# A mixture of experts written as 32 turns in a fixed order, its norms by a power on GpSimd, and an output projection booked one turn later

## The chip, the cores and the metric

The kernel runs on one core of one Trainium2 chip, alone. The metric is the device time of one execution in microseconds (us). Before the change three runs took 4461.84, 4466.29 and 4487.71 us; the median is 4466.29 us. All arithmetic named here is float32.

## The reference, cut to what matters

The network takes 2 sequences of 1024 tokens with 128 features (T = 2048 tokens) and runs eight stages, each adding its result to a residual stream: windowed attention (a0), a mixture of experts (ffn0), causal attention (b0), the mixture of experts again with the same weights, a pair attention (a1), then a six-layer local-attention transformer (ffn1), another pair attention (b1), and ffn1 again. The change touches a0 and both ffn0 stages. Each ffn0 normalises its input and then computes:

```python
logits = xt @ gate_w.T
scores = softmax(logits)                      # 8 experts
top_vals, idx = top_k(scores, 2)
weights = take_along_axis(scores, idx)
xs = xt[:, None, :] * weights[:, :, None]
for e in range(8):
    mask = (idx == e)
    h  = silu(xs @ w1[e].T + b1[e])
    x2 = h @ w2[e].T + b2[e]
    x3 = xs @ w3[e].T + b3[e]
    y  = y + sum(x2 * x3 * mask)
z = (silu(xt @ sw1.T) * (xt @ sw2.T)) @ sw3.T # shared part, 256 wide
out = y + z
```

In a0 the reference has 16 heads of 8 features, windows of 64 queries against 128 keys, a softmax, and an output projection `out @ Wo.T + bo`. The norm in front of each stage is (x - mean) / sqrt(var + 1e-5).

## The kernel before, in words

The residual stream stays in SBUF, features on partitions, as four tiles `xt[0..3]` of 128 x 512 (512 tokens each, a "block"). A stage opens its own tile pools. The stages follow each other because each reads what the last one added to `xt`.

**ffn0.** Every expert is computed for every token; unchosen ones are scaled by zero. Four parts, all in `ffn0`:

1. For each of the four blocks: `norm` (L107) = `norm_in` (four transposes L115, statistics L119 and L120 on DVE, square root on ACT L126 and its reciprocal on DVE L127, scaling L130) and `norm_out` (transposes L139, copy to SBUF by ACT L142); then the gate logits of the block (L238).
2. The choice of two experts for all 2048 tokens at once: a chain of some twenty small DVE instructions with one exponential on ACT (L252 to L271) that leaves weights and marks in `sel`.
3. For each block: the rows of `sel` for the block are transposed (L278) and copied (L282); the shared part (`s1`, `s2` by L289, Silu L297, product L298, `yz` L299) is added to `xt` (L300).
4. For each block and each four experts: L306 spreads the four weights over 128 partitions by four matmuls with 32 rows each, into four PSUM banks; L310 multiplies them with the normalised block (`xe`). For each pair: L316 starts two banks with the b3 rows (again 32-row matmuls); then for each expert L321 adds w3, L289 makes h, L324 takes its Silu, L326 copies x3 to SBUF, L289 makes x2 from h, L328 (DVE) forms (x2 + b2) * x3, and L331 (GpSimd) adds it to `xt`. One block-and-expert is called a unit here; there are 32 in a stage.

All this is emitted in program order, but the order on each engine is the planner's: outside a manual schedule the framework places an instruction where its priorities and buffers allow, so the shared part of a later block and single spreads of L306 land between the experts of an earlier one. PSUM has eight banks: two pools of four ("m" and "tp"). The SBUF pool holds three buffers for h and for x3, six for xe.

**a0.** After the projections, `Chunks.run` walks 16 chunks of 128 queries in software-pipelined turns, inside a manual schedule: there PE, ACT, DVE and GpSimd execute exactly in the written order. Turn n holds both halves of the softmax of chunk n, the transposes of chunk n-2, the sums of n-1, the scores of n+1 and the outputs of n-2. In `outputs`, every fourth chunk (m % 4 == 3) also projects four finished chunks: matmuls L668 into `a0y`, and L670 on DVE adds the result to `xt`. The softmax's subtractions (L625, L626), L633 and L670 share DVE's queue in that order.

GpSimd's queue carries the normalisation of a0 (L636), the memset of `sel` (L251) and the 64 additions L331. SP's queue issues DMAs only, none of them inside these loops.

Of the kernel before, what the change touches and what calls it, by code (L numbers as in the profile page):

```python
# [10 lines left out]
F32 = mybir.dt.float32  # L11
BF16 = mybir.dt.bfloat16
AF = mybir.ActivationFunctionType
ALU = mybir.AluOpType
# [3 lines left out]
P = 128  # L18
# [28 lines left out]
class Net:  # L47
    def __init__(self, ctx, tc, t):
# [7 lines left out]
        self.nc.gpsimd.memset(self.eps, EPS)  # L56

# [53 lines left out]
    def norm_in(self, src, ps, key, tag="tp", by_exp=False):  # L111
        nc = self.nc
        tp = ps.tile([P, 4, P], F32, tag=tag, name=f"ln_in_{key}")
# [8 lines left out]
        if by_exp:  # L122
            nc.scalar.activation(rs, mv[:, :, 1], AF.Ln, bias=self.eps)
            nc.scalar.activation(rs, rs, AF.Exp, scale=-0.5)
        else:
            nc.scalar.activation(rs, mv[:, :, 1], AF.Sqrt, bias=self.eps)  # L126
            nc.vector.reciprocal(rs, rs)  # L127
        xn = self.lnp.tile([P, 4, P], F32, tag="ln_xn", name=f"ln_xn_{key}")
# [6 lines left out]
    def norm_out(self, xn, dst, ps, key, gain=None, bias=None, tag="tp"):  # L135
        nc = self.nc
        tq = ps.tile([P, 4, P], F32, tag=tag, name=f"ln_out_{key}")
# [78 lines left out]
    def ffn0(self, key):  # L216
        nc, tc = self.nc, self.tc
        NT = T // P
        with ExitStack() as ctx:
            cp = ctx.enter_context(tc.tile_pool(name=f"f0c_{key}", bufs=1))  # L220
            sb = ctx.enter_context(tc.tile_pool(name=f"f0s_{key}", bufs=3))
            ps = ctx.enter_context(tc.tile_pool(name=f"f0ps_{key}", bufs=4, space=PSUM))
            w, wsel = self.w["f0"], self.w["f0_sel"]
            w123 = w[:, 0 : 3 * E * P].rearrange("p (s e h) -> p s e h", s=3, e=E)
            o = 3 * E * P
            sw1, sw2, sw3 = (w[:, ds(o + 256 * i, 256)] for i in range(3))
            gate = w[:, ds(o + 768, E)]
            b1, b2 = w[:, ds(o + 776, E)], w[:, ds(o + 784, E)]
            desc = w[:, ds(o + 792, E)]
            spread, b3 = wsel[:, 0], wsel[:, 1]  # L230

            xn = []
            lg = ps.tile([P, NT, E], F32, tag="m", name=f"lg_{key}")
            for k in range(NBLK):
                x = cp.tile([P, 512], F32, tag=f"xn{k}", name=f"f0xn_{key}_{k}")
                self.norm(self.xt[k], x, ps, f"{key}_{k}")
                for c in range(4):
                    nc.tensor.matmul(lg[:, 4 * k + c, :], x[:, ts(c, P)], gate, start=True, stop=True)  # L238
                xn.append(x)


            def tl(name, shape=(P, NT, E)):
                return cp.tile(list(shape), F32, tag=name, name=f"{name}_{key}")

            def over_e(v):
                return v[:, :, None].to_broadcast([P, NT, E])

            s, m = tl("s"), tl("m", (P, NT))

            sel4 = tl("sel", (P, NT, 4, 32))  # L250
            nc.gpsimd.memset(sel4, 0.0)  # L251
            nc.vector.tensor_reduce(m, lg, AX.X, ALU.max)  # L252
            nc.vector.tensor_tensor(s, lg, over_e(m), ALU.subtract)
            nc.scalar.activation(s, s, AF.Exp)
            nc.vector.tensor_reduce(m, s, AX.X, ALU.add)
            nc.vector.reciprocal(m, m)
            nc.vector.tensor_tensor(s, s, over_e(m), ALU.mult)
            one, two, cand, rest = tl("one"), tl("two"), tl("cand"), tl("rest")
            dbc = desc[:, None, :].to_broadcast([P, NT, E])
            for left, hot in ((s, one), (rest, two)):  # L260
                nc.vector.tensor_reduce(m, left, AX.X, ALU.max)
                nc.vector.tensor_tensor(cand, left, over_e(m), ALU.is_equal)
                nc.vector.tensor_tensor(cand, cand, dbc, ALU.mult)
                nc.vector.tensor_reduce(m, cand, AX.X, ALU.max)
                nc.vector.tensor_tensor(hot, cand, over_e(m), ALU.is_equal)
                if hot is one:
                    nc.vector.scalar_tensor_tensor(rest, one, -4.0, s, ALU.mult, ALU.add)
            nc.vector.tensor_tensor(one, one, two, ALU.add)
            nc.vector.tensor_tensor(s, one, s, ALU.mult)
            for v, lo in ((s, 0), (one, E)):  # L270
                nc.vector.tensor_copy(  # L271
                    sel4[:, :, :, lo : lo + E], v[:, :, None, :].to_broadcast([P, NT, 4, E])
                )

            for k in range(NBLK):
                tp = ps.tile([P, 4, P], F32, tag="tp", name=f"f0ts_{key}_{k}")
                for c in range(4):
                    nc.tensor.transpose(  # L278
                        tp[:, c, :], sel4[:, 4 * k + c].rearrange("p r e -> p (r e)"), self.ident
                    )  # L280
# [3 lines left out]
                def bank(name, tag="m"):  # L284
                    return ps.tile([P, 512], F32, tag=tag, name=f"f0{name}_{key}_{k}")
# [940 lines left out]
```

## Time and profile before

| what | us |
|---|---|
| median of three runs | 4466.29 |
| the profiled execution, device time | 4471.09 |
| its span | 4469.3 |
| mean granted TensorE clock | 0.939 |
| a0's turns, from the first full turns to the last addition to `xt` | about 86 to 239.6 |
| first ffn0, from its first transpose to the first of b0 | 239.66 to 424.33 (184.7) |
| second ffn0, from its first transpose to the first of a1 | 519.31 to 704.35 (185.0) |
| busy in the span: PE, DVE, ACT, GpSimd | 3964.8, 3480.8, 2385.2, 1983.1 |

The two ffn0 stages are 370 of 4469 us; most of the rest is ffn1, which the change leaves alone. Times inside the span are counted from its start. PE busy time is the union of modelled matmul intervals, so a busy PE isn't a PE at its fastest; distances from start to start of matmuls tell more. A float32 matmul of 512 columns shows as two records (two passes). "Idle before" names what ended the wait of an engine.

### The profile page before, as it was taken

The numbers are of one execution on the slowest core, as the hardware profiler recorded it, in microseconds if no ns is written. First come the engines' busy times: TensorE is split into PE (matmuls) and PEld (weight loads), VectorE is DVE, ScalarE is ACT, GpSimd is POOL, SyncE is SP. The second block draws the span as 40 slices with busy tenths as digits, with TensorE's granted clock in tenths as the row PEclk, the third lists the DMA queues.
The fourth block names the chain that finished last, engine by engine and source line by source line (L and its number), as shares of the span: only waits on it lengthen the run. The fifth ranks groups of instructions, "written<-read, shape, count | busy, mean of one in ns | idle before, by whom it ended". The sixth has DMA issues, their size and how long they took to land. (4 is left out here: it accounts for less than half of the span.)

```text
span 4469.3 us, 149599 instructions
## 1 busy us (share of the span) xinstructions
PE 3964.8 (89%) x64920; PEld 2604.5 (58%) x64920; DVE 3480.8 (78%) x5605; ACT 2385.2 (53%) x4319; POOL 1983.1 (44%) x1175
## 2 busy tenths in 40 slices
PE   7788796799999999999999847999999999999998
PEld 4533433566666666666666535666666666666665
DVE  6733535788888888888889657888888889888896
ACT  3433232565565565656566416655656656565654
POOL 1322022545555455555554215455554555554552
PEclk8689898899999999999999868999999999999998
DMA  1000000223223232232222102222232322322222
GB/s 53 2 1 0 1 0 19 80 68 78 70 68 85 63 83 72 65 82 66 68 64 63 45 19 80 65 76 71 68 83 67 84 69 70 83 63 68 61 64 52
DMA packets 181539, 261.09 MB, mean 58 GB/s; under 512 B 51100, under 2 KB 74264, under 8 KB 180632
## 3 DMA queue, kind: packets, MB, share of 16 engines
q1 hardware_dynamic: 180888, 251.52, 22.0%
q8 instruction: 517, 8.47, 0.8%
q14 instruction: 134, 1.10, 0.1%
HBM read 52.09 MB, written 1.05 MB: 12 GB/s over the span
## 5 line engine op out<-in xcount | busy, mean ns | idle before, releaser
L846 DVE TENSOR_TENSOR t_l<-pj_l,rot_l 128x512 f32<-128x512 f32 x1536 | 963.6, 681 | 315.3 <-ACT sq_l L843 200.2
L856 POOL TENSOR_TENSOR raw_l<-t_l,t_l 128x1024 f32<-128x1024 f32 x384 | 908.1, 2365 | 513.5 <-DVE t_l L846 495.0
L839 PE MATMUL pj_l<-wqkv_l,x_l 128*128 128x512 f32 x1536 | 846.1, 634 | 63.0 <-DVE t_l L846 58.5
L868 POOL TENSOR_TENSOR raw_l<-raw_l,rn_l 128x1024 f32<-128x1024 f32 x384 | 724.1, 1907 | 145.8 <-ACT rn_l L866 145.8
L985 PEld LDWEIGHTS av_l<-pT_l,vw_l 64*64 64x64 f32 x24576 | 460.6, 137 | 263.7 <-issue 134.6
L985 PE MATMUL av_l<-pT_l,vw_l 64*64 64x32 f32 x24576 | 491.5, 223 | 108.8 <-issue 85.4
L886 PEld LDWEIGHTS tqk_l<-ident_sb,raw_l 128*128 128x128 f32 x3072 | 387.0, 147 | 343.2 <-issue 289.5
L843 ACT ACTIVATE sq_l<-pj_l 128x512 f32<-128x512 f32 x768 | 459.6, 599 | 209.1 <-PE pj_l L839 207.4
L886 PE MATMUL tqk_l<-ident_sb,raw_l 128*128 128x128 f32 x3072 | 497.7, 287 | 40.2 <-POOL raw_l L868 26.1
L891 POOL COPY kT_l<-kT_l 128x256 f32<-128x256 f32 x168 | 77.4, 461 | 985.5 <-ACT kT_l L888 985.5
L852 DVE TENSOR_REDUCE ss_l<-sq_l 128x16 f32<-128x1024 f32 x384 | 465.7, 1213 | 5.7
L958 DVE TENSOR_TENSOR pr_l<-pr_l,sm_l 128x1024 f32<-128x1024 f32 x192 | 400.6, 2087 | 6.6
L904 PE MATMUL pv_l<-wqkv_l,x_l 128*128 128x512 f32 x768 | 391.9, 593 | 0.1
L1012 PE MATMUL y_l<-outT_l,wo_l 128*128 128x128 f32 x3072 | 375.6, 276 | 2.1 <-DVE t_l L846 2.1
L839 PEld LDWEIGHTS pj_l<-wqkv_l,x_l 128*128 128x128 f32 x1536 | 256.2, 197 | 197.9 <-issue 113.8
L1012 PEld LDWEIGHTS y_l<-outT_l,wo_l 128*128 128x128 f32 x3072 | 359.6, 192 | 4.9 <-DVE t_l L846 2.6
L973 ACT COPY pT_l<-tpr_l 128x512 f32<-128x512 f32 x384 | 211.0, 589 | 241.2 <-PE tpr_l L969 237.3
L993 ACT COPY outT_l<-av_l 128x512 f32<-128x512 f32 x384 | 207.2, 590 | 213.5 <-PE av_l L985 213.4
L946 DVE TENSOR_REDUCE mx_l<-sc_l 128x8 f32<-128x512 f32 x384 | 263.4, 686 | 72.5 <-PE sc_l L941 69.5
L941 PEld LDWEIGHTS sc_l<-kT_l,qT_l 64*32 64x32 f32 x24576 | 258.3, 105 | 86.4 <-issue 85.4
L941 PE MATMUL sc_l<-kT_l,qT_l 64*32 64x64 f32 x24576 | 290.6, 226 | 2.2 <-issue 2.1
L888 ACT COPY kT_l<-tqk_l 128x512 f32<-128x512 f32 x384 | 224.2, 585 | 110.5 <-PE tqk_l L886 109.6
(337 smaller groups left out, 5732.4 us busy)
## 6 DMA issues: line engine op xcount, KB each, us to landing
vw_l<-v_l SPq DMA_DIRECT2D x3024, 64.0 KB, 2.0
wqkv_l<-in_Wqkv SPq DMA_DIRECT2D x36, 512.0 KB, 4.2
rot_l<-in_rotary SPq DMA_DIRECT2D x24, 512.0 KB, 4.0
wo_l<-in_Wo SPq DMA_DIRECT2D x12, 512.0 KB, 8.8
w_l<-in_W SPq DMA_DIRECT2D x12, 341.0 KB, 3.5
f_sb<-in_f SPq DMA_DIRECT2D x1, 1936.0 KB
qks_l<-in_qk_scale SPq DMA_DIRECT2D x12, 128.0 KB, 3.1
w_l<-in_W SPq DMA_DIRECT2D x12, 128.0 KB, 3.9
```

The source lines that it names most:

```text
L839: nc.tensor.matmul(pj.rearrange("p h d -> p (h d)"), self.x[b][0][:, ts(a, P)], self.w[i]["qkv"][:, ds(INNER * s + 512 * u, 512)], start=T ...
L843: nc.scalar.activation(sq[:, u], pj, AF.Square)
L846: nc.vector.tensor_tensor(to, pj, tabs[:, k, None, ts(w, LD // 2)].to_broadcast(half), ALU.mult)
L852: nc.vector.tensor_reduce(st["ss"][:, ts(s, LH)], st["sq"].rearrange("p u h d -> p h u d"), AX.XY, ALU.add)
L856: nc.gpsimd.tensor_tensor(r.rearrange("p h u d -> p u h d"), st["t1"], st["t2"], ALU.add)
L868: nc.gpsimd.tensor_tensor(r, r, rn[:, ts(s, LH), None].to_broadcast([P, LH, LD]), ALU.mult)
L886: nc.tensor.transpose(tp[:, j, :], flat[:, ts(4 * c + j, P)], self.ident)
L904: nc.tensor.matmul(pj, self.x[b][0][:, ts(a, P)], self.w[i]["qkv"][:, ds(2 * INNER + 512 * r, 512)], start=True, stop=True,)
L941: nc.tensor.matmul(sc[j][ts(c, 32), hp, :], st["q"][rows, hp, ts(c, 32)], st["k"][rows, hp, ds(32 * c, 64)], start=False, stop=(hp == 7),)
L958: nc.vector.tensor_tensor(p3, p3, sm[:, :, None].to_broadcast([P, 16, 64]), ALU.mult)
L985: nc.tensor.matmul(av[r][64 * j : 64 * j + 64, q, ts(c, 32)], st["vw"][rows, c, ts(2 * q + j, LD)], st["pT"][j][rows, q, ts(c, 32)], start ...
L1012: self.nc.tensor.matmul(y[:, 0:P], self.w[i]["o"][:, c, :], st["o"][:, c, :], start=(c == 0), stop=(c == 7))
```

## The change

Three things change; the arithmetic is the same but for how 1/sqrt(var + eps) is formed in ffn0.

- ffn0 becomes a class `Experts` under a manual schedule for the four engines. A prologue handles the four blocks with norm statistics, norm application and logits staggered by a block, with the shared part of blocks 0 and 1 in between; then the choice; then the shared parts of blocks 2 and 3. A loop of 33 turns follows: turn u makes h of unit u, x2 of unit u-1 and x3 of unit u; spreads come four together at every fourth turn. PSUM is split "b" 4, "x3" 2, "h" 1, "x2" 1 bank; h and x3 have four SBUF buffers, xe eight.
- In ffn0's norms the ACT square root and DVE reciprocal give way to two GpSimd instructions, an addition of eps and a power of -0.5. Other stages keep theirs.
- a0's projection leaves `outputs` for a stage `project`, called a turn later, after the first half of the softmax.

```diff
+        elif how == "power":
+            nc.gpsimd.tensor_scalar_add(rs, mv[:, :, 1], EPS)
+            nc.gpsimd.tensor_tensor(rs, rs, self.nhalf, ALU.pow)
...
         do(self.scores, 0)
-        for n in range(last + 2):
+        for n in range(last + 3):
             do(self.softmax, n, 0)
+            do(self.project, n - 3)
             do(self.transposes, n - 2, 0)
...
+    def bank(self, tag, name):
+        bufs = {"b": 4, "x3": 2, "h": 1, "x2": 1}[tag]
+        return self.ps.tile([P, 512], F32, tag=tag, name=f"f0{name}_{self.key}", bufs=bufs)
+
+    def run(self):
+        self.lg = self.ps.tile([P, T // P, E], F32, tag="x2", name=f"lg_{self.key}")
+        st = {}
+        for k in range(NBLK + 1):
+            if 2 <= k < NBLK:
+                self.shared_in(k - 2)
+            if k < NBLK:
+                st[k] = self.net.norm_stats(
+                    self.net.xt[k], self.ps, f"{self.key}_{k}", "b", "power", bufs=4
+                )
+            if 1 <= k <= NBLK:
+                xn = self.net.norm_mid(st.pop(k - 1), f"{self.key}_{k - 1}")
+            if 2 <= k < NBLK:
+                self.shared_out(k - 2)
+            if 1 <= k <= NBLK:
+                self.logits(k - 1, xn)
+        self.choice()
+        for k in range(2, NBLK):
+            self.shared_in(k)
+        self.to_rows(0, "x2")
+        for k in range(2, NBLK):
+            self.shared_out(k)
+        self.to_rows(1)
+        self.spreads(0)
+        self.scaled(0, 2)
+        self.scaled(2, 4)
+        last = NBLK * E
+        for u in range(last + 1):
+            if u < last:
+                self.first(u)
+            if u > 0:
+                self.second(u - 1)
+            if u < last:
+                self.third(u)
+                more = u // 4 * 4 + 4 < last
+                if u % 4 == 1 and more:
+                    self.spreads(u // 4 + 1)
+                    self.scaled(u + 3, u + 5)
+                if u % 4 == 2 and more:
+                    self.scaled(u + 4, u + 6)
+                if u % E == 7 and 1 < u // E + 2 < NBLK:
+                    self.to_rows(u // E + 2)
...
+    def shared_in(self, k):
+        nc, xn = self.nc, self.xs[k]
+        gs = self.h["shared", k] = []
+        for c in range(2):
+            p1 = self.mm("x3", f"s1{k}{c}", self.sw1[:, ts(c, P)], xn)
+            p2 = self.mm("b", f"s2{k}{c}", self.sw2[:, ts(c, P)], xn)
+            g = self.sb.tile([P, 512], F32, tag="h", name=f"f0g_{self.key}_{k}_{c}", bufs=4)
+            nc.scalar.activation(g, p1, AF.Silu)
+            nc.vector.tensor_tensor(g, p2, g, ALU.mult)
+            gs.append(g)
...
+    def first(self, u):
+        e = u % E
+        ph = self.mm("h", f"h{u}", self.w123[:, 0, e, :], self.xe[u])
+        h = self.h[u] = self.sb.tile([P, 512], F32, tag="h", name=f"f0h_{self.key}_{u}", bufs=4)
+        self.nc.scalar.activation(h, ph, AF.Silu, bias=self.b1[:, e : e + 1])
+
+    def third(self, u):
+        nc, e, sT = self.nc, u % E, self.sT[u // E]
+        if u % 2 == 0:
+            for d in range(2):
+                self.x3[u + d] = self.bank("x3", f"x3{u + d}")
+            for d in range(2):
+                r = (e + d) % 4
+                rows = slice(32 * r, 32 * r + 32)
+                nc.tensor.matmul(
+                    self.x3[u + d], self.b3[rows, e + d, :], sT[rows, :], start=True, stop=False
+                )
+        p3 = self.x3[u]
+        nc.tensor.matmul(p3, self.w123[:, 2, e, :], self.xe.pop(u), start=False, stop=True)
+        x = self.x3[u] = self.sb.tile([P, 512], F32, tag="x3", name=f"f0x3_{self.key}_{u}", bufs=4)
+        nc.scalar.copy(x, p3)
+
+    def second(self, u):
+        nc, e, x3, xt = self.nc, u % E, self.x3.pop(u), self.net.xt[u // E]
+        p2 = self.mm("x2", f"x2{u}", self.w123[:, 1, e, :], self.h.pop(u))
+        nc.vector.scalar_tensor_tensor(x3, p2, self.b2[:, e : e + 1], x3, ALU.add, ALU.mult)
+        nc.gpsimd.tensor_tensor(xt, xt, x3, ALU.add)
```

Not shown: `norm_stats` and `norm_mid` are the two halves of the old `norm_in`; `logits` is `norm_out` plus the gate matmuls; `choice` is the old chain unchanged; `shared_out` is `yz` in the single "h" bank and its addition; `to_rows` is L278 and L282 in a "b" bank; `spreads` is four L306 matmuls into the four "b" banks, `scaled` is L310; `project` is L668 and L670 unchanged.

## The prediction

> **What bounds the kernel now.** I read the page's first part, then the table of windows, because the stages follow each other and the shares of the whole span say little about 370 us of it.
>
> ```profile
> PE 3964.8 (89%) x64920; PEld 2604.5 (58%) x64920; DVE 3480.8 (78%) x5605; ACT 2385.2 (53%) x4319; POOL 1983.1 (44%) x1175
> ```
>
> ```profile
> core 0: us, PE busy (x) PEld busy (x) DVE busy (x) ACT busy (x) POOL busy (x), PEclk, DMA share, GB/s
> ...
> 86.00:239.70 153.70, 114.95 (x2016) 84.76 (x2003) 107.64 (x140) 67.65 (x103) 58.18 (x31) 0.71 0.01 2
> 239.70:274.00 34.30, 21.83 (x80) 13.93 (x80) 18.12 (x74) 9.47 (x15) 0.00 (x0) 0.66 0.00 0
> ...
> 553.00:705.00 152.00, 145.50 (x373) 50.96 (x372) 51.77 (x74) 48.10 (x75) 39.77 (x32) 1.00 0.00 0
> ```
>
> The first ffn0 is a prologue of 34 us in which no engine is full and the clock is 0.66, then an expert loop of 150 us with PE busy 96% at full clock (the last line is the second ffn0's loop). So PE sets the loop; the question is how much of its busy time is needed. The timeline of PE over the last pair of units tells:
>
> ```profile
> 695.68 1.13 PE L316 MATMUL f0x_e<-f0sT_e,f_sel_sb 32*128 32x512 f32 x4
> 696.74 1.13 PE L321 MATMUL f0x_e<-f0x_e,f_sb 128*128 128x512 f32 x2
> 697.70 1.02 PE L289 MATMUL f0h_e<-f0x_e,f_sb 128*128 128x512 f32 x2
> 698.56 1.02 PE L321 MATMUL f0x_e<-f0x_e,f_sb 128*128 128x512 f32 x2
> 699.56 1.12 PE L289 MATMUL f0x_e<-f0h_e,f_sb 128*128 128x512 f32 x2
> 700.52 1.02 PE L289 MATMUL f0h_e<-f0x_e,f_sb 128*128 128x512 f32 x2
> 702.38 1.12 PE L289 MATMUL f0x_e<-f0h_e,f_sb 128*128 128x512 f32 x2 [0.84 <-ACT f0h_e L324]
> ```
>
> From start to start a full matmul (x2, two passes) takes 0.86 (697.70 to 698.56). A group of 32-row matmuls takes 1.06, whether two or four share it, and the full matmul after it 0.96. The step 700.52 to 702.38 is 1.86: 1.00 is a wait for the Silu of the same unit. The waits of the same window add:
>
> ```profile
> ACT f0x_e L326 <- POOL xt L331: 37.0, 11, 3.6
> DVE f0x_e L310 <- PE f0b_e L306: 14.8, 19, 2.2
> PE f0x_e L289 <- ACT f0h_e L324: 5.7, 9, 0.8
> ```
>
> ACT holds x3 copies back for a free x3 buffer, and L306's spreads come one at a time. In a0, DVE is the fullest engine per turn, and stands still at the projection (timeline of DVE):
>
> ```profile
> 109.43 0.25 DVE L634 RECIPROCAL a0sm<-a0sm 128x16 f32<-128x16 f32 x1
> 118.71 0.75 DVE L670 SCALAR_TENSOR_TENSOR xt<-a0y,a_sb,xt 128x512 f32<-128x512 f32 x1 [9.03 <-PE a0y L668]
> 119.38 0.68 DVE L625 TENSOR_REDUCE a0mx<-a0sc 128x4 f32<-128x512 f32 x1
> ```
>
> **What the Trainium skill says.** "TensorEngine Tiling (Array Packing)", Tiling Modes: a change of the tiling mode drains TensorE. The trace agrees: 1.06 for the group instead of 0.86, and 0.10 on the matmul after it. "TensorE: Matmul & The Clock Gate", Part 1: the array runs at half clock until about 3.4 us of sustained activity. The trace agrees in kind: passes of 0.85 us in the prologue, 0.43 in the loop; PE busy from 244.86 is at full speed at about 250.3, 5.4 us. "ScalarE: Activation LUTs", Table sets: exp and sqrt lie in different table sets, each switch a load; the trace has 1.28 us a load, less than the page's 2.7. "GPSIMD Engine Reference", Instruction dispatch: a first call into a freshly loaded library costs about 6 us once; no run here shows it.
>
> **The change, part by part.** Sums are against the profiled execution, 4471.09 us (span 4469.3), 0.1% above the median 4466.29.
>
> *Loop of ffn0.* The new order is written out, so I count PE. Per pair of units: six full matmuls, 6 x 0.86 = 5.16, and one b3 group: 1.06 + 0.10 after + 0.09 on the last pass before it (a pass next to a switch starts its follower after 0.52 instead of 0.43) = 1.25. Sum 6.41; 16 pairs 102.6. Seven spread groups of four, 1.25 each, 8.75; two transposed row blocks of four 0.11 passes, about 1.0. Loop: 112.3, to the end of the last x2. Does anything make PE wait? h(u) needs the single h bank: Silu(u-1) starts 0.2 after h(u-1) ends, takes 0.69, ends at 1.75 from h's start, and h(u) comes at 2.58 at the earliest: slack 0.8. x2(u) needs the x2 bank: L328 ends 0.2 + 0.75 after x2(u-1), PE is back after 1.72 at least: slack 0.77. Where two L310 (2 x 0.69) lie ahead of L328 on DVE, a spread group has lengthened the turn by 1.25: still free. b3 needs both x3 banks: the copy (0.59) ends 0.8 after x3, PE comes after 1.72. GpSimd has 1.26 per unit of 3.5. The memset of `sel` (1.80) lies on GpSimd under the choice. So no wait is expected; the Silu is covered by three matmuls now instead of one.
>
> *Prologue*, walked from the stage's first transpose, durations from the prologue before. Two blocks' transposes 1.3, statistics 1.24 + 1.24 on DVE: 3.25. The scaling of block 0, 1.37; last transpose and copy 0.59: 5.8. Logits at half clock 1.88: 7.7. Shared part of block 0, eight passes, five cold (4.25), three warm (1.3): 12.8 (PE only); the second product 0.2 + 0.69 holds DVE's queue: 13.7. Behind it statistics of block 2 and scaling of block 1, 2.6: 16.3; transposes and copy 17.35; logits 0.95: 18.3. Shared part of block 1 3.45 and product: 22.7. Statistics 3, scaling 2, addition of `yz`, scaling 3: 27.4. Transposes, copy, logits of block 3: 29.8. If the clock falls back while DVE leads, up to 4.5 more; I take 32. Then the choice, 6.8 as before (262.68 to 269.46), covers the eight shared matmuls of blocks 2 and 3 (6.9 warm): 38.8. After it: four products 2.8 with the first `yz` (1.7) under the last two; its addition 0.69; the second `yz` behind the one bank 1.7; transposes 0.45; spreads 1.06; one L310 0.69; four hand-overs of 0.2: 7.8. First h at 46.6, against spreads at 34.4 before: the shared part moves here.
>
> *Stage.* 46.6 + 112.3 + 1.05 for the last L328 and the next stage's start = 160.0, against 184.7 and 185.0 now. Saved: 24.7 + 25.0 = 49.7.
>
> *GpSimd's power.* Removed per block: ACT 0.30, DVE 0.18, two hand-overs. Added: two GpSimd instructions on 128x4. No row shows a power. Lower bound the smallest memset, 0.10; nearest row a 128x48 product, 0.27 (L442); upper 1.26 (the 512-wide addition), and 6 us once by the skill. I take 0.3 each: statistics of block 1 (1.24) cover them. With 1.26 each, about 1.3 per stage shows. Below nothing is excluded: nothing waits for ACT there but table loads, off the path. Sqrt's table loads go; they were mostly hidden.
>
> *a0.* PE's order is unchanged: between `outputs` and the next transposes no PE work lies. DVE puts four softmax instructions (110.3 to 113.0, 2.7 us) in front of L670, where it stands idle anyway until 118.71; ACT's exponential follows at 113 instead of 122.3, so the copies behind it in ACT's queue start earlier. What is late next is L670 itself, which still waits for L668 (5.94, cold). Behind it on DVE queue the second half and the sums. Gain 2.7 for each of three projections (waits 9.03, 8.39 and, of 39.8 in all with 14.74 for the last, 7.6), the fourth has nothing to overlap: 8.1. Lower bound 0, if PE sets these turns.
>
> Sum: 49.7 + 8.1 = 57.8. 4471.1 - 57.8 = 4413.3, a ratio of 0.9871; on the median, 4408.
>
> **The rivals.**
>
> *Loop at a coarser beat.* With one bank each for h and x2, half a microsecond of waits per turn would remain: 33 x 0.5 x 2 = 33 lost, 4441, no measurable change. For it: the slacks are 0.8 and rest on hand-overs of 0.2. Against: such hand-overs are what the trace has (L324 starts 0.22 to 0.28 after its matmul). Chance 0.20, with a cold prologue in it.
>
> *a0 gives nothing*, since PE's cold L668 and transposes set the turn: 4408 + 8 = 4416, still faster by over 1%; inside the forecast.
>
> *Slower: the power is slow.* The place is DVE's queue: the scaling of block 0, with everything of the stage behind it, waits for GpSimd. With X us for a power, 2 to 4 of a stage's four are exposed, as the shared parts hide the rest: for X from 1.7 to 8.7, 2X - 2.3 a stage. Beyond, a third shows, 3X - 11: two stages lose 57.8 at X = 13.3. At X = 25 the loss is 128: 4536. For it: no row shows the instruction. Against: 128x4 is tiny, and GpSimd's smallest rows are 0.1 to 0.3. Chance 0.04.
>
> **How the numbers follow.** Forecast 0.76, coarser beat 0.20, slower 0.04. Forecast range: prologue 4 each way a stage, loop +4 or -2 a stage, a0 0 to 10: 4394 to 4424. The range reaches towards the second case: 4392 to 4440. One per cent (4421.6) is about what a measurement of this kernel can tell from no change. Of the forecast's 0.76 some 0.03 lie above it: faster 0.73, same 0.23, slower 0.04.
>
> **What would show it.** Loop: PE starts 6.4 apart per pair, first h to last x2 about 112, idle at L760 and L693 near zero. Prologue: first h near 46.6 after the first transpose. Power: L132 at 0.3. a0: DVE's wait at the projection 9.03 down to about 6.3, the next sums some 3 us earlier. Wrong if PE shows waits for ACT or DVE in the loop, if the clock in the loop falls under 0.95, or if L132 takes microseconds.

## The result, and the profile after

Four runs of the changed kernel took 4400.35 to 4411.44 us, median 4409.74; four of the kernel before, on the same terms, 4461.84 to 4487.71, median 4471.31. The ratio is 0.9854 (95% interval 0.982 to 0.9888): faster by 1.5%. The forecast was 4408. The profiled execution took 4411.22 us (span 4409.4), 59.9 us of span less than the one before. Stage by stage, read as in the table of before:

| stretch | before | after | gained | forecast |
|---|---|---|---|---|
| up to the first transpose of the first ffn0 (a0 within) | 239.66 | 225.34 | 14.3 | 8.1 |
| first ffn0, to the first transpose of b0 | 184.7 | 165.4 | 19.2 | 24.7 |
| b0 | 95.0 | 94.7 | 0.3 | 0 |
| second ffn0, to the first transpose of a1 | 185.0 | 165.0 | 20.0 | 25.0 |
| the rest, a1 to the end, unchanged code | 3764.9 | 3758.9 | 6.0 | 0 |

So the total was met by parts that were not: ffn0 gave 39.2 instead of 49.7, a0 gave 14.3 instead of 8.1, and 6.0 came from code that nobody touched.

The page's first part, and the table of windows for the prologue of the first ffn0 and both loops (columns as in the lines of before):

```profile
PE 3919.5 (89%) x64728; PEld 2594.5 (59%) x64920; DVE 3480.6 (79%) x5597; ACT 2376.8 (54%) x4307; POOL 1993.5 (45%) x1192
```

```profile
core 0: us, PE busy (x) PEld busy (x) DVE busy (x) ACT busy (x) POOL busy (x), PEclk, DMA share, GB/s
...
225.34:276.97 51.63, 43.51 (x129) 22.40 (x129) 25.55 (x82) 12.45 (x18) 6.80 (x9) 0.80 0.00 0
276.97:389.70 112.73, 112.58 (x320) 42.16 (x320) 42.38 (x62) 42.12 (x67) 38.99 (x31) 1.00 0.00 0
536.60:649.40 112.80, 112.62 (x321) 42.16 (x320) 42.47 (x63) 42.10 (x67) 39.00 (x31) 1.00 0.00 0
```

The loops are solid: PE busy 112.6 of 112.7 us at full clock. The prologue is not: 43.5 of 51.6, at 0.80. The timeline of PE over the last pair of units answers the seven lines shown of before:

```profile
642.62 1.02 PE L693 MATMUL f0x_e<-f0h_e,f_sb 128*128 128x512 f32 x2
643.57 1.13 PE L756 MATMUL f0x_e<-f0sT_e,f_sel_sb 32*128 32x512 f32 x4
644.62 1.13 PE L760 MATMUL f0x_e<-f0x_e,f_sb 128*128 128x512 f32 x2
645.59 1.02 PE L693 MATMUL f0h_e<-f0x_e,f_sb 128*128 128x512 f32 x2
646.45 1.02 PE L693 MATMUL f0x_e<-f0h_e,f_sb 128*128 128x512 f32 x2
647.30 1.02 PE L760 MATMUL f0x_e<-f0x_e,f_sb 128*128 128x512 f32 x2
```

No line has a wait behind it; start to start the full matmuls take 0.86 (645.59 to 646.45), the b3 group 1.05, its neighbours 0.95 and 0.97: the cadence that the prediction counted with. Only the stage's last x2, behind these lines, comes late, by 0.31: the one x2 bank is read until 648.32, and it starts at 648.47. The prologue shows what it had not counted. First PE's timeline, then DVE's, around the shared part of block 1:

```profile
239.44 1.88 PE L711 MATMUL f0yz_e<-f0g_e,f_sb 128*128 128x512 f32 x4
241.94 1.28 PE L152 MATMUL ln_out_e<-ident_sb,ln_xn_e 128*128 128x128 f32 x4 [0.61 <-DVE ln_xn_e L143]
243.90 1.60 PE L650 MATMUL lg_e<-f_sb,f0xn_e 128*128 128x8 f32 x8 [0.68 <-ACT f0xn_e L155]
245.35 6.50 PE L693 MATMUL f0s_e<-f0xn_e,f_sb 128*128 128x512 f32 x8
```

```profile
237.49 0.69 DVE L704 TENSOR_TENSOR f0g_e<-f0s_e,f0g_e 128x512 f32<-128x512 f32 x1 [6.86 <-PE f0s_e L693]
239.28 0.69 DVE L704 TENSOR_TENSOR f0g_e<-f0s_e,f0g_e 128x512 f32<-128x512 f32 x1 [1.09 <-PE f0s_e L693]
...
241.50 1.33 DVE L143 TENSOR_SCALAR ln_xn_e<-ln_in_e,ln_mv_e,ln_rs_e 128x128 f32<-128x128 f32 x4
```

DVE stands idle for 6.86 us, does the two products, then the statistics of block 2 (left out), and only then, at 241.50, the scaling of block 1, whose last input, GpSimd's power, ended at 230.8. "PSUM — Partial Sum Buffer", Engine vs sequencer instructions, has DVE's queue as strictly first in, first out, and these lines agree. PE waits 0.61 for it and 0.68 for the copy, and its clock falls: eight shared passes take 6.50 us, 3.45 in the forecast.

### The profile page after: what moved, and what is told of

Read it like the earlier page. It is cut to its first block, busy times and chain, and to the rows that moved or that the text cites. A ratio compares the mean times of both kernels' runs of the same rounds, so it can differ in the third digit from the quotient of the medians.

```text
span 4409.4 us, 149383 instructions
## 1 busy us (share of the span) xinstructions
PE 3919.5 (89%) x64728; PEld 2594.5 (59%) x64920; DVE 3480.6 (79%) x5597; ACT 2376.8 (54%) x4307; POOL 1993.5 (45%) x1192
## 3 DMA queue, kind: packets, MB, share of 16 engines
HBM read 52.09 MB, written 1.05 MB: 12 GB/s over the span
## 5 line engine op out<-in xcount | busy, mean ns | idle before, releaser
L986 ACT COPY kT_l<-tqk_l 128x512 f32<-128x512 f32 x384 | 224.1, 584 | 112.8 <-PE tqk_l L984 111.9
## 6 DMA issues: line engine op xcount, KB each, us to landing
qks_l<-in_qk_scale SPq DMA_DIRECT2D x12, 128.0 KB, 3.1
w_l<-in_W SPq DMA_DIRECT2D x12, 128.0 KB, 2.3
```

## The experiments

Each run is compared by the stretches of its trace, since the whole is a poor measure of a few microseconds: the unchanged rest after the second ffn0 took between 3739.3 and 3764.9 us in the fourteen profiled executions, and the medians of the kernel before, run beside each group of experiments, lay between 4459.2 and 4466.2. "First h" and "choice" are counted from a stage's first transpose, "loop" from the first h to the end of the last x2 (its start plus 0.86). Line numbers differ between the kernels by the lines that an edit adds; the tile names stay.

| kernel | last addition of a0 | choice, stages 1, 2 | first h | loop | stage | median us |
|---|---|---|---|---|---|---|
| before | 238.85 | 23.0, 22.9 | 37.4, 37.4 | 146.2, 146.5 | 184.7, 185.0 | 4471.31 |
| changed | 224.53 | 35.5, 35.4 | 51.6, 51.2 | 112.65 | 165.4, 165.0 | 4409.74 |
| a0_back | 235.75 | 35.5, 35.3 | 52.6, 51.1 | 112.65 | 166.4, 164.9 | 4421.33 |
| root_norms | 225.78 | 38.0, 35.0 | 54.8, 51.4 | 112.65 | 168.6, 165.2 | 4409.79 |
| planner_order | 225.82 | 30.0, 28.6 | 43.8, 42.4 | 112.65 | 157.6, 156.2 | 4393.93 |
| norms_first | 220.26 | 26.0, 26.0 | 54.2, 54.3 | 112.65 | 168.0, 168.1 | 4404.30 |
| scale_early | 225.81 | 30.9, 28.8 | 46.8, 44.5 | 112.65 | 160.6, 158.3 | 4395.05 |
| fill | 219.82 | 32.5, 32.3 | 47.1, 47.0 | 112.65 | 160.9, 160.8 | 4399.69 |
| singles | 225.94 | 35.5, 35.4 | 51.8, 51.2 | 132.2 | 185.1, 184.4 | 4444.42 |
| before_skew | 230.45 | 23.0, 23.1 | 37.3, 37.7 | 129.0 | 167.4, 167.8 | 4416.90 |
| before_bufs | 229.36 | 23.0, 22.9 | 37.3, 37.4 | 146.2, 146.5 | 184.6, 185.0 | 4463.32 |
| skew_a0 | 226.56 | 23.1, 23.2 | 37.4, 37.8 | 129.0 | 167.5, 167.8 | 4409.31 |
| skew_three | 218.83 | 23.0, 23.1 | 37.3, 37.6 | 129.0 | 167.4, 167.7 | 4404.08 |
| combined | 219.83 | 27.2, 26.2 | 41.6, 40.3 | 112.55 | 155.3, 154.0 | 4382.14 |

**What the fixed order is worth (planner_order).**

```diff
             experts = Experts(ctx, self, key)
-            with self.tc.manual_schedule(engines=ORDERED):
-                experts.run()
+            experts.run()
```

> The changed kernel with Experts run outside the manual schedule: same text, same PSUM banks and buffers, the order on the engines left to the planner. Theory (skew of a unit, one spread group at a time and the split of the banks are what shortens the loop; the planner has nothing to choose among then): first h to last x2 112 to 114 us, as with the fixed order; stage 162 to 168. Rival (the fixed order itself shortens the loop, the planner would pull h and x2 together again): loop 118 us or more, stage over 171.

The loop is the same to a hundredth, 112.65, and the stages are 8 to 9 us *shorter*, 157.6 and 156.2, below even what the theory left room for. The fixed order doesn't make the loop, and it costs in the prologue. PE's timeline there, with the same instructions as in the changed kernel's lines above:

```profile
241.47 1.88 PE L710 MATMUL f0yz_e<-f0g_e,f_sb 128*128 128x512 f32 x4
243.19 0.60 PE L152 MATMUL ln_out_e<-ident_sb,ln_xn_e 128*128 128x128 f32 x4
244.46 1.06 PE L649 MATMUL lg_e<-f_sb,f0xn_e 128*128 128x8 f32 x8 [0.67 <-ACT f0xn_e L155]
245.37 3.68 PE L692 MATMUL f0s_e<-f0xn_e,f_sb 128*128 128x512 f32 x8
```

The order on PE is the same here; the wait of 0.61 for the scaling is gone, the clock stays up, and the shared passes take 3.68.

**Queue or clock (scale_early, fill).** The first moves the scaling ahead on DVE's queue and leaves PE's order; the second leaves every queue and puts unused matmuls into PE's gaps.

```diff
+        xn = {}
         for k in range(NBLK + 1):
...
+            for j in {1: (0, 1), 2: (2,), 3: (3,)}.get(k, ()):
+                if j > 1:
+                    self.shared_out(j - 2)
+                xn[j] = self.net.norm_mid(st.pop(j), f"{self.key}_{j}")
             if 1 <= k <= NBLK:
-                xn = self.net.norm_mid(st.pop(k - 1), f"{self.key}_{k - 1}")
-            if 2 <= k < NBLK:
-                self.shared_out(k - 2)
-            if 1 <= k <= NBLK:
-                self.logits(k - 1, xn)
+                self.logits(k - 1, xn.pop(k - 1))
```

> The changed kernel, fixed order kept, with only DVE's queue altered in the prologue: the scaling of a block stands ahead of the previous block's shared products instead of behind them (and behind the addition of yz where there is one). TensorE's order is as in the changed kernel. Theory (the place of the scaling on DVE's queue is what the fixed order loses: TensorE stands still for it after yz, and its clock falls for the shared part behind): shared matmuls of block 1 in 3.7 us instead of 6.5, choice starts at 29 to 31 us instead of 35.5, first h at 45 to 47 instead of 51.6, stage 159 to 161, total 9 to 13 us under the changed kernel. Rival (the planner's order gained elsewhere, by statistics in a better order and by products between the steps of the choice): choice at 33 to 35, stage 163 to 165, total within 5 us.

```diff
+    def fill(self, k, part, n):
+        for i in range(n):
+            self.mm("x3", f"fill{k}{part}{i}", self.sw1[:, 0:P], self.net.w["f0"][:, 0:512])
...
+        self.fill(k, 0, 2 if k == 0 else 1)
         self.net.norm_out(xn, x, self.ps, f"{self.key}_{k}", tag="b", bufs=4)
+        self.fill(k, 1, 0 if k == 0 else 1)
```

> The changed kernel with filler matmuls (128x512, result unused) in TensorE's gaps of the prologue: two ahead of the first ln_out of a stage, one ahead of each later ln_out and of each later logits; DVE's and ACT's order as changed. It adds work and takes nothing away. Theory (half of the 5 us missed is clock, not queue): shared matmuls of block 1 in 3.5 to 4 us instead of 6.5, those of blocks 2 and 3 in 7 instead of 9.1, first h 47 to 49 instead of 51.6, stage 161 to 163. Rival (the queue on DVE alone; fillers cost their own time, some 0.25 us each past the gap, 6 of them): first h 52 to 54, stage 166 to 168.

Both theories hold. With the scaling early, the choice starts at 30.9 and 28.8 and h at 46.8 and 44.5 (the second stage a little better than expected): 4.8 and 6.8 of the 7.8 and 8.9 us that the planner's order won; the rest was not taken apart. With fillers, h comes at 47.1 and 47.0, 4.5 and 4.2 earlier, most of the 5 us missed and not half, though each filler is extra work. PE's timeline with fillers, block 1:

```profile
235.08 1.88 PE L717 MATMUL f0yz_e<-f0g_e,f_sb 128*128 128x512 f32 x4
236.80 1.02 PE L699 MATMUL f0fill_e<-f_sb 128*128 128x512 f32 x2
237.66 1.20 PE L152 MATMUL ln_out_e<-ident_sb,ln_xn_e 128*128 128x128 f32 x4
238.70 1.02 PE L699 MATMUL f0fill_e<-f_sb 128*128 128x512 f32 x2
239.56 1.04 PE L656 MATMUL lg_e<-f_sb,f0xn_e 128*128 128x8 f32 x8
240.45 3.68 PE L699 MATMUL f0s_e<-f0xn_e,f_sb 128*128 128x512 f32 x8
```

The queues are as in the changed kernel, and the shared passes take 3.68 instead of 6.50: so those 2.8 us were clock. The shared passes of blocks 2 and 3 went from 9.11 to 7.11 as well. The place on DVE's queue matters mainly because it opens the gap of 0.61 ahead of the one of 0.68. With both gaps, the shared passes of block 1 took 5.38 to 6.61 us in all six stages of the changed kernel, a0_back and singles. Without the first, they took 3.68 in all eight of planner_order, scale_early, fill and combined, though three of these keep the second. The gap doesn't cost clock every time: one stage of root_norms, below, has a wider gap and 3.68.

**Norms first.** The obvious other order, all norms ahead of all shared parts:

```diff
-            if 2 <= k < NBLK:
-                self.shared_in(k - 2)
...
-            if 2 <= k < NBLK:
-                self.shared_out(k - 2)
...
         self.choice()
-        for k in range(2, NBLK):
+        for k in range(NBLK):
             self.shared_in(k)
+            if k == 1:
+                self.shared_out(0)
+                self.shared_out(1)
```

> The changed kernel with all four norms and logits ahead of any shared part; the shared parts of blocks 0 and 1 run under the choice, those of 2 and 3 after it. Theory (the shared parts of blocks 0 and 1 put their products ahead of the next norm on DVE's queue, and run at half clock, so the choice starts late): choice starts at about 16 us after the stage's start instead of 35.5, first h at 40 to 44 instead of 51.6; stage 154 to 158; total 15 to 23 us under the changed kernel. Rival (TensorE has to do the same matmuls anyway and does them at half clock under the choice, having stood nearly idle before it): first h at 47 to 52, stage 161 to 166, total within 9 us.

The theory failed and the rival was still too kind to the order: the choice starts at 26.0, not 16, h at 54.2, and the stages are 168 us. (The total lies under the changed kernel's for what a0 and the rest did in this run.) DVE's timeline tells why:

```profile
225.03 1.33 DVE L143 TENSOR_SCALAR ln_xn_e<-ln_in_e,ln_mv_e,ln_rs_e 128x128 f32<-128x128 f32 x4
230.49 0.30 DVE L124 BATCH_NORM_STATS2 ln_st_e<-ln_in_e 128x6 f32<-128x128 f32 x1 [4.12 <-PE ln_in_e L120]
```

The statistics of block 2 wait 4.12 us for that block's transposes, which stand on PE's queue behind the logits of block 0, which wait for ACT's copy, which waits for the scaling. In a written order each block's norm now ran one after the other, 7.0 us a block, and PE at half clock beside it. Behind the choice all four shared parts are left, so that h follows after 28.2 us, against 16.1 in the changed kernel. I had followed DVE's queue and not PE's.

**What shortens the loop (before_skew, before_bufs).** Back in the kernel before, with the planner's order, two pools and all the rest:

```diff
-                            p2 = mm(f"x2{e}", w123[:, 1, e, :], h)
-                            nc.vector.scalar_tensor_tensor(
-                                x3, p2, b2[:, e : e + 1], x3, ALU.add, ALU.mult
-                            )
-                            nc.gpsimd.tensor_tensor(self.xt[k], self.xt[k], x3, ALU.add)
+                            late.append((k, e, h, x3))
+                            if len(late) > 1:
+                                second(*late.pop(0))
+            second(*late.pop(0))
```

where `second` holds the four removed statements, and h and x3 have four buffers (the shared part's g, which has h's tag, too).

> The kernel before with x2 of a unit issued one unit later and four buffers for h and x3; pools, planner, norms and a0 as before. Theory (TensorE's waits for the Silu, 4.6 and 5.7 us in the two loops, are the part that the skew removes; the rest of the gain is fewer groups of 32-row matmuls and the shared parts leaving the loop): loops 146.3 to about 141, stage about 180, total 8 to 12 us under the kernel before. Rival (the skew makes the whole gain of the loop, as spreads and x3 then find their banks free): loop 134 or less, total 24 us or more under.

The rival won, by more than it claimed: the loops fell by 17.2 and 17.5 us to 129.0 and the stages by 17.3, with the shared parts of three blocks, 17.1 us, still inside. Without these that is 111.9. One b3 group and one x3, some 2 us, stand ahead of this loop's first h and behind the changed kernel's; with them the two loops, 113.9 and 112.65, are the same to about 1 us. The end of the loop on PE's timeline:

```profile
393.12 1.02 PE L279 MATMUL f0x_e<-f0h_e,f_sb 128*128 128x512 f32 x2
393.98 1.02 PE L329 MATMUL f0x_e<-f0x_e,f_sb 128*128 128x512 f32 x2
394.84 1.02 PE L297 MATMUL f0h_e<-f0x_e,f_sb 128*128 128x512 f32 x2
395.70 2.07 PE L279 MATMUL f0x_e<-f0h_e,f_sb 128*128 128x512 f32 x4
```

Every step is 0.86; the last row holds the x2 of two units (the 128.0 that the next expectation names leaves out the second of them). I had expected 5 us, the waits for the Silu as the view of waits has them. Where the rest was shows when the distances from each PE record's start to the next are summed by kind over the first loop. From before to before_skew, the steps that begin at h went from 33.2 to 27.6, at x2 from 31.5 to 28.5, at a spread from 12.8 to 7.2, at x3 from 30.0 to 28.2, at the transposed rows from 3.0 to 1.3; b3 rose from 18.3 to 18.8, the shared part stayed at 17.1. The groups of 32-row matmuls fell from 27 to 19; at the 1.22 us that a group is found to cost below, an estimate of 9.8 of the 17.2. In the loop of before, an x2 is not ready right behind its h, and the planner had put in what it found: an x3 behind 15 of the 32 h, a single spread behind eight, both behind one, the transposed rows and then a wait behind three, and behind five nothing but the wait. PE's timeline of the kernel before, early in the first loop:

```profile
280.85 1.02 PE L289 MATMUL f0h_e<-f0x_e,f_sb 128*128 128x512 f32 x2
281.80 1.12 PE L306 MATMUL f0b_e<-f0sT_e,f_sel_sb 32*128 32x512 f32 x2
282.85 1.12 PE L289 MATMUL f0x_e<-f0h_e,f_sb 128*128 128x512 f32 x2
283.91 1.13 PE L316 MATMUL f0x_e<-f0sT_e,f_sel_sb 32*128 32x512 f32 x4
```

The filler is a single spread, two records, with a tiling switch on either side: 2.00 us from h to x2. Eleven such lone spreads lie in this loop, eight of them in this place. The wait was filled, so the view of waits showed 5.4 us, under a third of the 17.2 that the order cost.

```diff
-                            h = sb.tile([P, 512], F32, tag="h", name=f"f0h_{key}_{k}_{e}")
+                            h = sb.tile([P, 512], F32, tag="h", name=f"f0h_{key}_{k}_{e}", bufs=4)
...
-                            x3 = sb.tile([P, 512], F32, tag="x3", name=f"f0x3_{key}_{k}_{e}")
+                            x3 = sb.tile([P, 512], F32, tag="x3", name=f"f0x3_{key}_{k}_{e}", bufs=4)
```

The shared part's g has four buffers here, too.

> The kernel before with four buffers for h and x3 instead of three, and nothing else. In the run of the kernel before with a skewed x2 and four buffers the loops took 128.0 us instead of 146.3; this tells the buffers from the skew. Theory (the skew does it; ACT's waits for GpSimd, 37 us in the loop before, lie beside the path): loops 144 to 147 us, total within 5 us of the kernel before. Rival (ACT's late copies of x3 hold TensorE's banks, so that spreads come one at a time; the fourth buffer frees them): loops 136 or less, total 20 us or more under.

Buffers alone change nothing: ratio to before 1.0009 (0.9999 to 1.0019), loops 146.2 and 146.5. And ACT's wait, which I had laid to the number of x3 buffers, is still there with a fourth (the view of waits of that kernel's first loop; 37.0, 11, 3.6 before):

```profile
ACT f0x_e L326 <- POOL xt L331: 37.1, 11, 3.6
```

The first of these eleven copies, with PE's x3 matmul and GpSimd's addition next to it (timelines of the three engines):

```profile
284.47 0.58 ACT L326 COPY f0x_e<-f0x_e 128x512 f32<-128x512 f32 x1 [3.59 <-POOL xt L331]
283.25 1.13 PE L321 MATMUL f0x_e<-f0x_e,f_sb 128*128 128x512 f32 x2
283.20 1.27 POOL L331 TENSOR_TENSOR xt<-xt,f0x_e 128x512 f32<-128x512 f32 x1 [1.36 <-DVE f0x_e L328]
```

The wait is for PE. In the first loop of both kernels each of the eleven copies starts 0.09 us after the end of the x3 matmul that it copies, as do most copies whose wait is put down to PE. GpSimd's addition of the unit before ends 0.00 to 0.02 ahead of the copy, by the cadence of the loop, and so was named as the cause; the buffer that the copy fills was read by an addition three or four units back.

**The price of a tiling switch (singles).**

```diff
-        if u % 2 == 0:
-            for d in range(2):
-                self.x3[u + d] = self.bank("x3", f"x3{u + d}")
...
+        self.x3[u] = self.bank("x3", f"x3{u}")
+        rows = slice(32 * (e % 4), 32 * (e % 4) + 32)
+        nc.tensor.matmul(self.x3[u], self.b3[rows, e, :], sT[rows, :], start=True, stop=False)
```

> The changed kernel with the b3 matmul of each unit by itself, ahead of its own x3, instead of two together ahead of the pair: the same matmuls, 16 more groups of 32-row matmuls a stage. Theory (a group costs 1.25 us over the full matmuls around it, whether one, two or four share it): loop 112.65 + 16 x 1.25 = 132.6, stage 185.4, total 40 us more than the changed kernel. Rival (the matmuls of a group run one after the other and only the switch is shared, 0.4 us): loop 112.65 + 16 x 0.4 = 119.1, total 13 us more.

132.21 us in both loops: 19.56 for 16 more groups, 1.22 each, against 1.25 in the prediction. PE's timeline, a unit's b3 alone:

```profile
679.98 1.02 PE L693 MATMUL f0x_e<-f0h_e,f_sb 128*128 128x512 f32 x2
680.93 1.12 PE L752 MATMUL f0x_e<-f0sT_e,f_sel_sb 32*128 32x512 f32 x2
681.99 1.12 PE L754 MATMUL f0x_e<-f0x_e,f_sb 128*128 128x512 f32 x2
682.95 1.02 PE L693 MATMUL f0h_e<-f0x_e,f_sb 128*128 128x512 f32 x2
```

One matmul takes the 1.06 (680.93 to 681.99) that two took. "TensorEngine Tiling (Array Packing)", Key Properties, says that tiles work in parallel and a change of mode drains; the runs agree with both, and here a lone group costs as much as a full one.

**The projection of a0 (a0_back, and the pair before_bufs and skew_three).**

```diff
-        for n in range(last + 3):
+        for n in range(last + 2):
             do(self.softmax, n, 0)
-            do(self.project, n - 3)
...
             do(self.outputs, n - 2)
+            do(self.project, n - 2)
```

> The changed kernel with the projection of a0 put back at the end of its turn (called right after outputs), the rest as changed. Theory (the softmax's first half fills DVE's wait; 2.7 us for each of three projections, 8.1, and the clock of TensorE at the first projection gave the other 6 of the 14.3 us seen): the last addition of a0 to xt starts at 232 to 234 us if the first projection's matmuls run at full clock (some 3.7 us), at 237 to 239 if they run at half clock (5.9 us); DVE's waits before that addition come back to 8 to 9 us each; total 8 to 14 us above the changed kernel. Rival (the move itself also keeps the clock up, since no wait follows it): always 238 to 239, half clock at the first projection. ffn0 unchanged by either: 165 us a stage, within 1.

The last addition lies at 235.75, 11.2 us later than in the changed kernel, and the total is 11.6 us higher. The addition misses both ranges of the theory: the first two projections were slow (6.03 and 5.39 us) and the third was not (3.70), with DVE's waits at 9.12, 8.48 and 5.10. So this run doesn't measure the move at equal clock. In two other runs all four projections ran at full clock, 3.70 us each: before_bufs, whose a0 is that of before, and skew_three (below), whose a0 is the changed one. DVE's timeline at the first projection of before_bufs, then of skew_three:

```profile
114.64 0.75 DVE L670 SCALAR_TENSOR_TENSOR xt<-a0y,a_sb,xt 128x512 f32<-128x512 f32 x1 [5.10 <-PE a0y L668]
...
123.81 0.69 DVE L625 TENSOR_REDUCE a0mx<-a0sc 128x4 f32<-128x512 f32 x1 [0.58 <-PE a0sc L613]
```

```profile
114.42 0.75 DVE L680 SCALAR_TENSOR_TENSOR xt<-a0y,a_sb,xt 128x512 f32<-128x512 f32 x1 [2.44 <-PE a0y L678]
...
120.21 0.63 DVE L633 TENSOR_REDUCE a0mx<-a0sc 128x4 f32<-128x512 f32 x1
```

The wait falls by 2.66, the forecast's 2.7, and the next wait for scores, 0.58, goes as well, since the scores then start earlier. From one projection's addition to the next is 43.46, 38.50 and 32.76 us in the one, 40.02, 35.08 and 29.31 in the other: 3.4 each, 10.5 in all at the last addition (229.36 to 218.83). It is the move and not the clock elsewhere in these turns: between the first two additions the granted clock is 0.69 in before_bufs, 0.79 in skew_three and 0.70 in fill, which has the changed a0 and takes 40.02 like skew_three. The rival, that the move keeps the clock up, has no support: the first projection was slow in seven of the ten profiled executions with the move and in three of the four without. The same code of a0 ended at 238.85 in the profile of before and at 229.36 in before_bufs; that range is the clock's. "TensorE: Matmul & The Clock Gate", Part 1, says that the window which decides the clock runs freely, so that the number of slow matmuls changes from run to run; the projections here, 3.70 or 5.2 to 6.8 us in the same code, agree.

**The power (root_norms).**

```diff
-                    self.net.xt[k], self.ps, f"{self.key}_{k}", "b", "power", bufs=4
+                    self.net.xt[k], self.ps, f"{self.key}_{k}", "b", "root", bufs=4
```

> The changed kernel with ffn0's norms by ACT's square root and DVE's reciprocal again, inside the fixed order. Theory (the statistics of the next block cover either way of forming the root): each ffn0 stage within 2 us of 165.4, total within 4 us. Rival (in a fixed order the table loads for Sqrt, Silu and Exp, 1.28 us each, fall between the norms and the Silus on ACT's queue, four or more of them on the path): 5 to 8 us a stage more, total 10 to 16 us more.

The second stage is the same within 0.2 us and the first 3.1 longer, just past the theory's 2; the median is the changed kernel's. On the queues both stages lose the same: two table loads fall between a Silu and the next square root, DVE's reciprocal of block 1 stands ahead of block 0's scaling, and PE's three waits for a scaling are 4.41, 1.16 and 1.16 us in the first stage, against 3.31, 0.61 and 0.62 in the changed kernel, 2.2 more (2.2 in the second stage, too). What differs is the clock. PE's timeline in the second stage:

```profile
503.92 1.29 PE L152 MATMUL ln_out_e<-ident_sb,ln_xn_e 128*128 128x128 f32 x4 [1.16 <-DVE ln_xn_e L143]
505.88 1.06 PE L650 MATMUL lg_e<-f_sb,f0xn_e 128*128 128x8 f32 x8 [0.68 <-ACT f0xn_e L155]
506.80 3.68 PE L693 MATMUL f0s_e<-f0xn_e,f_sb 128*128 128x512 f32 x8
```

The shared passes of block 1 take 3.68 here and 5.90 in the first stage, 6.20 and 6.50 in the changed kernel. So the second stage won back by clock what it lost on the queues, and the theory held there by luck. The power's own time, from the instructions of the changed kernel's L132 (ns, minimum, median, maximum):

```profile
L132 POOL TENSOR_TENSOR ln_rs_e<-ln_rs_e,nhalf x8: 1025/1034/1037, 228.2 to 514.4; 128x4 f32<-128x4 f32 x8
```

1.03 us, three times my 0.3, and within the bounds; the next block's statistics cover it, barely: block 0's power ends at 229.23, and DVE comes to the scaling at 229.30. None of the eight shows the dearer first call that the prediction kept in its bounds.

**The gain from two small edits (skew_a0, skew_three).** If the skew and the projection are the gain, the kernel before with just these should be as fast as the changed one.

> The kernel before with x2 one unit later, four buffers for h and x3, and the projection of a0 one turn later; no class, no fixed order in ffn0, no power, the shared parts of blocks 1 to 3 still in the loop. Theory (these two edits are the whole gain of the change; the fixed order, the power and the new prologue sum to about nothing): stage 167.5 us as with the skew alone, last addition of a0 at 220 to 226 us, total 4400 to 4412. Rival (fixed order or power carry part of the gain): total over 4420.

> The kernel before with x2 one unit later and the projection of a0 one turn later, the three buffers for h and x3 kept: the two edits without the extra buffers. Theory (a skewed x3 tile lives from its copy to GpSimd's addition, some 2 units of 3.5 us, so three buffers still suffice, just): loops 128 to 129 us, stage 167 to 169, total 4400 to 4415. Rival (with three buffers ACT's copy waits for GpSimd's addition two units back, and TensorE for its bank): loops 132 to 140, total 4420 to 4440.

skew_a0, the diff of before_skew with the projection of a0 moved as in the change, took 4409.31 us, the changed kernel's 4409.74 within its spread; skew_three, which keeps three buffers, 4404.08, its loops again 129.0. So class, fixed order, split of PSUM, eight `xe`, power and the staggered prologue sum to little, 2.1 and 2.8 us in the two stages. They are not nothing each: planner_order, the class without the fixed order, has stages 9.9 and 11.7 us shorter than skew_a0, and the fixed order takes back 7.8 and 8.9.

**A faster kernel (combined).** The changed kernel with the scaling early, five fillers about block 0's norm, and a tail that keeps PE fed:

```diff
         self.to_rows(0, "x2")
-        for k in range(2, NBLK):
-            self.shared_out(k)
-        self.to_rows(1)
+        self.shared_out(2)
         self.spreads(0)
         self.scaled(0, 2)
+        self.shared_out(3, "x2")
+        self.to_rows(1, "x3")
         self.scaled(2, 4)
```

> The changed kernel, fixed order kept, with the scaling of a block early on DVE's queue, five filler matmuls around block 0's ln_out to keep the clock up, and a tail in which the first spreads stand between the two yz of blocks 2 and 3, each yz in a bank of its own. Theory (queue place, clock and the single yz bank are what the prologue loses): choice at 27 to 28.5 us, first h at 40 to 42, loop 112.65, stage 153.7 to 156, total 18 to 23 us under the changed kernel. Rival (the gains of scaling and fillers are the same gain, since either keeps the clock up): first h 44 to 46, stage 158 to 160, total 11 to 15 us under.

First h at 41.6 and 40.3, stages 155.3 and 154.0, median 4382.14, a ratio to before of 0.9827 (0.9806 to 0.9847): 27.6 us under the changed kernel's median, of which the two stages account for 21.2, as the theory had it; the other 6 are within what the rest of the program varies by. PE's timeline at the start of the stage:

```profile
221.57 3.60 PE L698 MATMUL f0fill_e<-f_sb 128*128 128x512 f32 x8
225.05 1.28 PE L152 MATMUL ln_out_e<-ident_sb,ln_xn_e 128*128 128x128 f32 x4
226.17 1.02 PE L698 MATMUL f0fill_e<-f_sb 128*128 128x512 f32 x2
227.07 1.06 PE L655 MATMUL lg_e<-f_sb,f0xn_e 128*128 128x8 f32 x8
227.98 3.68 PE L698 MATMUL f0s_e<-f0xn_e,f_sb 128*128 128x512 f32 x8
```

The first shared part takes 3.68 us too, 5.54 in the changed kernel. These fillers stand at block 0 and not at block 1, where the early scaling closes the gap: so the two gains add up.

## Why the prediction was right, point by point

*Loop of ffn0: right.* 112.3 forecast, 112.65 measured. No wait of PE in it but the 0.31 ahead of the last x2, as the slacks of 0.8 said, so the rival of a coarser beat fell. The price per group, 1.25, measured 1.22. The count did not say which edit brings it; there I would have been wrong, as before_skew shows: I read the Silu waits as their whole price.

*A reading that fell:* "ACT holds x3 copies back for a free x3 buffer". With a fourth buffer the wait stands at 37.1, and the copies start when their x3 matmul ends: they wait for PE, which sets the loop. I took the name that the view gives for the cause.

*Prologue: wrong by 5.* First h at 51.6 and 51.2, forecast 46.6. The failed step is the walk's line "Shared part of block 1 3.45": it measured 6.50 and 6.20, most of it at half clock. The allowance "I take 32" for the choice covered 2.2 of this, and the choice came at 35.5 and 35.4. The rest is smaller: statistics of two blocks 3.2 instead of 2.5, as the fixed order alternates each pair (0.40 from pair to pair, 0.26 where the planner reorders), and 9.15 instead of 7.8 from the end of the choice to h. Two of the walk's sums are slips: 7.7, 4.25 and 1.3 make 13.25 and not 12.8, and the terms behind the choice make 8.2 and not 7.8. The walk had even named the cause: the product "holds DVE's queue", with statistics and scaling behind it. It priced the queue; for the clock it named up to 4.5 and allowed 2.2.

*Power: size wrong, place right.* 1.03 for 0.3, hidden; nothing on the path, so the slower rival fell. The words "nothing waits for ACT there" were too strong: in the kernel before, DVE's reciprocal waits 0.36 for the root, and with the root inside the fixed order PE waits 2.2 us a stage more.

*a0: mechanism right, size low.* The wait fell by 2.66 where the projection had the same clock, as said; the wait for the next scores went with it, another 0.8 each, 10.5 in place of 8.1. The remaining 3.8 of the 14.3 are the clock of the two executions compared. "a0 gives nothing" fell.

*The sum: right by luck in part.* 10.5 us missed in ffn0 came back as 6.2 in a0 and 6.0 in the rest of the program, of which 9.8 (3.8 and 6.0) is, as far as these runs show, no effect of the change; that these made good the miss is luck. At equal clock its worth is about 39.2 + 10.5 = 49.7 us, 4421 by the span's arithmetic; the medians differ by 61.6, and the interval of the ratio, 50 to 80 us, has its edge there. Against the medians of the kernel before beside the other groups, the changed kernel's is 49 to 56 us lower.

## What to carry to other kernels

A wait that a scheduler has filled with something worse is missing from the view of waits: look at what runs in its place and what that costs, here single tiling switches; the order cost three times the wait that the view showed. A name in that view can be a coincidence: compare the start of the waiting instruction with the ends of all that feed it. Try the one-line edit (an operation issued one unit later) before a rewrite, and split a rewrite before crediting its largest part. A written order must be walked queue by queue, PE's as well as DVE's: a late instruction in one opens a gap in the other, and a gap of 0.6 us on PE can cost 2 to 3 us of clock behind it (1.7 to 2.9 here, in six stages of six).

## What the runs showed of the hardware

A power on a 128x4 tile takes GpSimd 1.03 us, against 0.23 for the addition of a constant of the same size. A lone pair of 32-row passes costs TensorE 1.22 us among full matmuls, as much as four passes that share the group. Filling two gaps of 0.6 and 0.7 us with useless matmuls made the eight passes behind them 2.8 us shorter, yet in one stage with gaps of 1.2 and 0.7 us the passes were as short. And the part of the program that no edit touched differed by up to 26 us between profiled executions.
